# A graph attention layer: some of the gathered rows are loaded one by one from SP's queue

## The chip, the cores and the metric

The kernel runs on one core of a Trainium2 chip. A core has a matrix engine (PE, TensorE), a vector engine (DVE), a scalar engine (ACT), a general engine (POOL, GpSimd) and a sequencer for transfers (SP, SyncE). Each has its own queue of instructions, works it off in order, and waits on semaphores for the others. Transfers between the memory outside (DRAM) and the memory on the core (SBUF, 128 partitions) run on 16 DMA engines; SP, ACT and POOL start them. The metric is the device time of one execution in microseconds (us).

## The reference

One layer of graph attention over 12500 nodes and 412500 edges that are sorted by their target node. Cut to what matters:

```python
h = relu(layernorm(x)) @ W_node.T           # per node, 4 heads of 32
e = edge_attr @ W_edge.T                    # per edge
att = leaky_relu(sum([h[src], h[tgt], e] * a))
m = max(segment_max(att, tgt), 0)
ex = exp(att - m[tgt])
denom = segment_sum(ex, tgt) + (E - deg) * exp(-m)
out = x + segment_sum(ex / denom[tgt] * h[src], tgt)
```

The costly access is `h[src]`: for each of the 412500 edges a row of its source node, at an address that only the data tells.

## The kernel before

First a table is made in DRAM, one row per node: 144 floats (576 bytes) that hold h of the four heads, two columns of ones each, and the parts of the attention that belong to source and target. Then the edges are worked through in 58 batches. A batch has 8 chunks of 896 edges; a chunk has 7 tiles of 128 edges, so a full batch has 56 tiles (the last has 31; in all there are 3223).

Per batch, in the functions that follow:

- `index(b)` (L155) loads the batch's source and target indices, 128 partitions x 56 tiles each, from SP. It runs two batches ahead.
- `load(s)` (L404) starts from SP the edge features `eft` (L408), the target ids `mem` (L412, two loads), and eight small pieces of the table, `twb` (L418), whose addresses SP reads into registers first (`least_i`, L413).
- `gather(s)` (L431) lets POOL wait until `sums` is there (the copy to `gate`, L434) and then issues one indirect transfer per tile (L436): 128 rows of the table, one for each partition, at the 128 addresses in a column of `src`. The target is `hs`, a buffer that exists twice. `sums` belongs to the batch two before, whose `hs` buffer is used again.
- `begin(s)` (L445) multiplies `eft` and `mem` on PE into `z` (L454, L457) and makes the one-hot matrices `hot`. `eft` and `mem` have one buffer each, so the next `load` waits until these matmuls are done.
- `weigh(s)` (L478) takes the source part out of `hs` (L482, a transpose on DVE, which needs all rows of the batch) and computes the softmax weights with DVE and ACT. It reads `pen`, which `load_pen` (L440) loads from SP into a single buffer, after `weigh` of the batch before has read it.
- `scatter(s)` (L509) multiplies the rows by their weights (L520) and adds them up by target on PE (L527).
- `collect(s)` (L533) copies the sums out (L545), first of all the `sums` that POOL waits for (L537); `merge` joins two batches into `acc`.

The main loop (L688) gives the order by hand. In round b: the indices of batch b+2, `load` and `gather` of batch b+1, `weigh` of batch b, `load_pen` of batch b+1, `scatter` of batch b, `begin` of batch b+1, `collect` of batch b. `finish` adds x and stores an output part after some rounds. On SP's queue one round is therefore: two index loads, `eft`, two `mem`, the register load, eight `twb`, `pen`, and sometimes a store and a load of x.

A load that SP starts signals one of eight semaphores, which are taken in turn; the load that takes a semaphore again waits until the one eight before it has landed.

Of the kernel before, what the change touches and what calls it, by code (L numbers as in the profile page):

```python
# [12 lines left out]
I32 = mybir.dt.int32  # L13
AF = mybir.ActivationFunctionType
OP = mybir.AluOpType
AX = mybir.AxisListType
ENG = mybir.EngineType

P = 128
# [6 lines left out]
T = 7  # L26
CE = T * P
CT = 2 * T
NCH = -(-E // CE)
LAST = -(-(E - (NCH - 1) * CE) // P)  # L30
SB = 4
CB = 2 * SB
NBT = -(-NCH // CB)
# [8 lines left out]
NB = -(-N // P)  # L42
# [9 lines left out]
ROW = EROW + H  # L52
BUF = max(CE, MC * 2 * AW, CB * H * AW)
BANKS = 2
BIG = 2.0**100
EPS = 1e-5


def tiles_of(sc):

    return [T if c < NCH - 1 else LAST for c in (2 * sc, 2 * sc + 1) if c < NCH]
# [11 lines left out]
    return got  # L73


def groups_of(n):


    if n <= 4:
        return [(0, n, 0)]  # L80
    return [(0, 4, 0), (n - 4, 4, n - 4)]
# [3 lines left out]
def kernel(  # L85
    ctx: ExitStack,
    tc: tile.TileContext,
    x: bass.AP,
    src: bass.AP,
    dst: bass.AP,  # L90
    dstc: bass.AP,
    ef: bass.AP,
# [5 lines left out]
    nc = tc.nc  # L98
# [4 lines left out]
    table = dram.tile([NB * P, ROW], F32, name="table")  # L103
# [49 lines left out]
    indices = ctx.enter_context(tc.tile_pool(name="indices", bufs=3))  # L153

    def index(b):  # L155
        got = []
        for what, name in ((src, "src"), (dst, "dst")):
            t = indices.tile([P, SB * CT], I32, name=name)
            nc.sync.dma_start(t, what[:, b * SB * CT:(b + 1) * SB * CT])
            got.append(t)  # L160
        return got


    with (
# [13 lines left out]
        for g in range(NG):  # L178
            n = min(P, NC2 - g * P)
# [40 lines left out]
        def extent(g):  # L220
# [4 lines left out]
            pen = p2.tile([P, CE + 1], F32, name="pen", bufs=NG)  # L225
            nc.gpsimd.memset(pen, -BIG)
            yield
# [90 lines left out]
        early = []  # L318
        k = -4
        while k < 0 or line:  # L320
# [17 lines left out]
            if k == -2:  # L338
                early = [index(b) for b in range(2)]
# [2 lines left out]
            k += 1  # L342
        for _ in extents:
            pass
        pb = [pps.tile([P, NC2], F32, name=f"pb{k}", bufs=1) for k in range(2)]
        for k in range(2):
            for g in range(NG):
                n = min(P, NC2 - g * P)
# [35 lines left out]
        for a in range(4):  # L384
            r = slice(a * W, (a + 1) * W)
            nc.vector.tensor_scalar(nid[r, :], top[r, :].rearrange("p (b a) -> p b a", a=4)[:, :, a], rcol[r, :],
                                    None, op0=OP.add)
# [16 lines left out]
    def load(s):  # L404

        c0 = s.b * CB
        s.eft = work.tile([P, SB, CE], F32, name="eft")
        nc.sync.dma_start(s.eft, ef[s.b * SB:(s.b + 1) * SB, :, :].rearrange("j p e -> p j e"))  # L408
        s.mem = work.tile([P, 2, CE], F32, name="mem")
        for k in range(2):  # L410
            rows = dstc[c0 + 4 * k:c0 + 4 * k + 4, :]
            nc.sync.dma_start(s.mem[:, k, :].bitcast(I32), rows[:, None, :].to_broadcast([4, W, CE]))  # L412
        _, at = nc.values_load_multi_w_load_instructions(  # L413
            least_i[0:1, c0:c0 + CB], engines=[ENG.SP], min_val=0, max_val=NB * P - W,
            skip_runtime_bounds_check_because="a dst is at most N, and N + W at most NB * P")
        for i, v in enumerate(at):
            r = (i % 4) * W
            nc.sync.dma_start(twb[r:r + W, s.b % 2, i // 4, i * H:(i + 1) * H], table[ds(v, W), EROW:])  # L418
        s.hs = work.tile([P, SB * CT, ROW], F32, name="hs", bufs=2)
        s.tiles = []  # L420
        for t in range(T):
            for sc in range(s.b * SB, (s.b + 1) * SB):
                held = tiles_of(sc) + [0, 0]
                for c in range(2):
                    i = (sc - s.b * SB) * CT + c * T + t
                    if t < held[c]:
                        s.tiles.append(i)
                    else:
                        nc.vector.memset(s.hs[:, i, :], 0.0)

    def gather(s, sums=None):  # L431

        if sums is not None:
            nc.gpsimd.tensor_copy(gate, sums)  # L434
        for i in s.tiles:
            nc.gpsimd.indirect_dma_start(  # L436
                out=s.hs[:, i, :], out_offset=None, in_=table[:, :],
                in_offset=bass.IndirectOffsetOnAxis(ap=s.src[:, i:i + 1], axis=0))

    def load_pen(s):  # L440
        s.pen = work.tile([R, CE + 1], F32, name="pen")
        rows = pens[s.b * CB:(s.b + 1) * CB, :]
        nc.sync.dma_start(s.pen, rows[:, None, :].to_broadcast([CB, H, CE + 1]))
# [34 lines left out]
    def weigh(s):  # L478


        zst = work.tile([P, T, R], F32, name="zst")
        nc.vector.transpose(zst.rearrange("p t i -> p (t i)"),  # L482
                            s.hs[:, :, :EROW].rearrange("p (q t) (h k) -> p t q h k", t=T, h=H)[:, :, :, :, AW - 1])
        att = work.tile([P, BUF], F32, name="a")[:R, :CE]

        def grouped(what, g):
            return what.rearrange("r (t g i) -> r g t i", g=NQT, i=R)[:, g, :, :]

        for g in range(NQT):
            nc.vector.tensor_tensor(grouped(s.z, g), grouped(s.z, g), zst[g * R:(g + 1) * R, :, :], op=OP.add)  # L490
            nc.scalar.activation(grouped(att, g), grouped(s.z, g), AF.Identity, scale=0.2)  # L491
        nc.vector.tensor_tensor(s.z, s.z, att, op=OP.max)  # L492
        up = ps.tile([P, BANKS * 512], F32, name="up")[:R, :CE]
        nc.vector.tensor_tensor_scan(up, s.pen[:, :CE], s.z, 0.0, op0=OP.add, op1=OP.max)  # L494
        m = work.tile([P, BUF], F32, name="m")[:R, :CE]
        nc.vector.tensor_tensor_scan(m[:, ::-1], s.pen[:, CE:0:-1], up[:, ::-1], 0.0, op0=OP.add, op1=OP.max)  # L496
        nc.vector.tensor_tensor(att, s.z, m, op=OP.subtract)  # L497
        both = work.tile([P, 2, T, R], F32, name="both")
        for g in range(NQT):
            nc.scalar.activation(both[g * R:(g + 1) * R, 0, :, :], grouped(att, g), AF.Exp)  # L500
        for g in range(NQT):
            nc.vector.scalar_tensor_tensor(both[g * R:(g + 1) * R, 1, :, :], grouped(s.pen[:, 1:], g), -1.0 / BIG,  # L502
                                           grouped(m, g), op0=OP.mult, op1=OP.mult)
        s.ex, s.mx = exr
        for k, what in enumerate(exr):
            nc.vector.transpose(what.rearrange("p t r -> p (t r)"),
                                both[:, k, :, :].rearrange("p t r -> p (t r)"))
# [25 lines left out]
    def collect(s):  # L533

        n = s.chunks
        if s.b + 2 < NBT:
            nc.scalar.copy(sums, s.pa[:, CB // G - 1, 0:1])  # L537
        k = s.b % MB
        if k == 0:
            merged["r"] = work.tile([P, AW, MC + 1], F32, name="r")  # L540
        at = 1 + k * CB
        for g in range(min(n, G)):
            to = merged["r"][:, :, at + g:at + n:G]
            for h in range(H):
                nc.scalar.copy(to[h * W:(h + 1) * W, :, :],  # L545
                               s.pa[g * W:(g + 1) * W, :-(-(n - g) // G), h * AW:(h + 1) * AW]
                               .rearrange("p c d -> p d c"))
# [131 lines left out]
    def batch(b):  # L679
        if b not in batches:  # L680
            s = batches[b] = Batch()
            s.b = b
            s.chunks = min(CB, NCH - b * CB)
        return batches[b]

    stores = []
    with tc.manual_schedule():
        for b in range(-1, NBT):  # L688
            if b == -1:
                for k in range(2):  # L690
                    batch(k).src, batch(k).dst = early[k]
                load_pen(batch(0))
            elif b + 2 < NBT:
                batch(b + 2).src, batch(b + 2).dst = index(b + 2)
            if b + 1 < NBT:
                load(batch(b + 1))
                gather(batch(b + 1), sums if b >= 1 else None)
            if b >= 0:
                s = batch(b)
                weigh(s)  # L700
                if b + 1 < NBT:
                    load_pen(batch(b + 1))
                for store in stores:
                    store()
                stores.clear()
                scatter(s)
            if b + 1 < NBT:
                begin(batch(b + 1))
            if b >= 0:
                collect(batch(b))  # L710
                if (b + 1) % MB == 0 or b == NBT - 1:
                    g = b // MB
                    merge(g, min(MC, NCH - g * MC))
                del batches[b]
            if b == 3:
                count_windows()
            for b0, n, last in parts():
                if last == b:
                    stores.append(finish(work, ps, "up", em_ps, b0, n))
        for store in stores:  # L720
            store()
# [249 lines left out]
```

## Time and profile before

| | |
|---|---|
| time, median of 10 runs | 4199.71 us (4198.31 to 4200.48) |
| the profiled execution's own time | 4198.87 us |
| its span, first to last instruction | 4196.5 us |
| POOL busy | 3082.6 us (73%) |
| DVE busy | 1758.0 us (42%) |
| PE busy | 1110.6 us (26%), at a granted clock of 0.624 |
| ACT busy | 564.7 us (13%) |
| moved by DMA | 441.32 MB, mean 105 GB/s |
| by POOL's queue (gathers) | 237.83 MB, 21.6% of the 16 DMA engines' time |
| by SP's queue | 192.44 MB, 14.1% |

A row of the profile names the line, the engine, the operation and the tiles (written <- read), then count, busy time, mean duration and the idle time in front, with what ended it. Instructions with which SP starts a transfer are not counted as busy; they are shown in the time line and by line as SPq, their sequencer's queue, with the time that starting them took, not the transfer's. A wait names the instruction that ended it.

### The profile page before, as it was taken

Reading aid. Unit: us, or ns where it says so; the run is one execution under the profiler, and the core shown is the slowest. Engines: PE = TensorE matmul, PEld = TensorE weight load, DVE = VectorE, ACT = ScalarE, POOL = GpSimd, SP = SyncE. Lnnn points to the kernel's source line nnn. Section 1 sums busy time; section 2 is a strip of 40 time slices with the busy share of each in tenths; the row PEclk is TensorE's granted clock in tenths of the full one; section 3 lists DMA queues with packets and bytes.
Section 4 is the critical chain, followed back from the end, with each engine's and each line's share of the span. In section 5 each row is a group of like instructions: output and inputs, shape, how many; then the busy total and the mean of one; then the engine's idle time right before and its main releaser. Section 6 shows DMA issues by size and latency. Waiting matters only on the chain. (4 is left out here: it accounts for less than half of the span.)

```text
span 4196.5 us, 30865 instructions
## 1 busy us (share of the span) xinstructions
PE 1110.6 (26%) x8641; PEld 625.6 (15%) x8641; DVE 1758.0 (42%) x3450; ACT 564.7 (13%) x2149; POOL 3082.6 (73%) x3300
## 2 busy tenths in 40 slices
PE   6222222222222222222222223231222131313232
PEld 4011111111111111111111111111111111111111
DVE  7334453435343533343335333443343344433444
ACT  6011111111111111111111111111111111111111
POOL 2777777777777777777777777777777777777773
PEclk8566666566656565656566656565656565656566
DMA  5333433343433333434333334343333343433331
GB/s 165 110 114 89 130 98 113 93 118 89 118 93 114 98 114 93 118 88 118 93 114 98 114 93 118 89 118 94 113 98 114 93 118 89 118 93 114 98 115 40
DMA packets 243621, 441.32 MB, mean 105 GB/s; under 512 B 93914, under 2 KB 144086, under 8 KB 243446
## 3 DMA queue, kind: packets, MB, share of 16 engines
q0 software_dynamic: 103136, 237.83, 21.6%
q1 hardware_dynamic: 126486, 192.44, 14.1%
q10 hardware_dynamic: 13824, 9.02, 0.7%
q8 instruction: 72, 1.18, 0.1%
q14 instruction: 103, 0.84, 0.1%
HBM read 423.75 MB, written 15.29 MB: 105 GB/s over the span
## 5 line engine op out<-in xcount | busy, mean ns | idle before, releaser
L436 POOL DMA_INDIRECT hs<-table,src x3223 | 3049.0, 946 | 1056.3 <-issue 1052.0
L527 PE MATMUL pa<-hs,hot 128*32 128x140 f32 x6446 | 494.1, 341 | 2837.5 <-DVE hs L520 2808.4
L482 DVE STREAM_TRANSPOSE zst<-hs 128x224 f32<-128x224 f32 x58 | 33.6, 579 | 2003.4 <-DMA hs<-table,src 2003.4
L527 PEld LDWEIGHTS pa<-hs,hot 128*32 128x32 f32 x6446 | 408.7, 133 | 2946.6 <-DVE hs L520 2848.9
L520 DVE TENSOR_TENSOR hs<-hs,exr 128x924 f32<-128x924 f32 x461 | 478.0, 1108 | 50.7 <-ACT hs L514 50.7
L491 ACT ACTIVATE a<-z 32x224 f32<-32x224 f32 x232 | 80.3, 346 | 2364.5 <-DVE z L490 2364.5
L454 PE MATMUL z<-eft,wa 128*32 128x384 f32 (+1 forms) x928 | 361.9, 543 | 22.9 <-DMA twb<-table 22.9
L545 ACT COPY r<-pa 32x70 f32<-32x70 f32 x928 | 252.7, 272 | 27.8 <-PE pa L527 17.6
L457 PE MATMUL z<-mem,twb 128*32 128x512 f32 x464 | 186.3, 545 | 4.9 <-DVE key L465 4.9
L500 ACT ACTIVATE both<-a 32x224 f32<-32x224 f32 x232 | 89.9, 388 | 370.1 <-DVE a L497 365.9
L454 PEld LDWEIGHTS z<-eft,wa 128*32 128x32 f32 x928 | 97.7, 110 | 235.1 <-issue 228.8
L473 DVE TENSOR_TENSOR hot<-exr,key 128x448 f32<-128x448 f32 x231 | 128.0, 616 | 6.0
L490 DVE TENSOR_TENSOR z<-z,zst 32x224 f32<-32x224 f32 x232 | 89.8, 387 | 80.6 <-ACT a L491 75.2
L598 DVE TENSOR_TENSOR acc<-acc,a 128x70 f32 x461 | 107.4, 233 | 34.2 <-DVE acc L598 19.5
L494 DVE TENSOR_TENSOR_SCAN up<-pen,z 32x896 f32<-32x896 f32 x58 | 117.0, 2017 | 2.0
L496 DVE TENSOR_TENSOR_SCAN m<-pen,up 32x896 f32<-32x896 f32 x58 | 116.4, 2007 | 2.0
L502 DVE SCALAR_TENSOR_TENSOR both<-pen,m 32x224 f32<-32x224 f32 x232 | 88.1, 380 | 2.4
L537 ACT COPY sums<-pa 128x1 f32<-128x1 f32 x56 | 8.9, 159 | 580.9 <-PE pa L527 580.9
L663 PE MATMUL up<-a,ident 128*32 128x224 f32 (+2 forms) x480 | 44.9, 552 | 156.2 <-DVE a L656 156.2
L449 DVE TENSOR_SCALAR mem<-mem,nid 128x896 f32<-128x896 int32 x116 | 74.2, 680 | 21.3 <-issue 15.6
L492 DVE TENSOR_TENSOR z<-z,a 32x896 f32<-32x896 f32 x58 | 63.0, 1087 | 23.9 <-ACT a L491 23.9
L457 PEld LDWEIGHTS z<-mem,twb 128*32 128x32 f32 x464 | 51.4, 111 | 130.4 <-issue 110.0
(137 smaller groups left out, 860.7 us busy)
## 6 DMA issues: line engine op xcount, KB each, us to landing
eft<-in_ef SPq DMA_DIRECT2D x58, 1792.0 KB
mem<-in_dstc SPq DMA_DIRECT2D x116, 448.0 KB
hs<-table,src POOLq DMA_INDIRECT x3223
twb<-table SPq DMA_DIRECT2D x464, 0.5 KB
pen<-pens SPq DMA_DIRECT2D x58, 112.1 KB
table<-rows ACTq DMA_DIRECT2D x10, 648.0 KB
xg<-in_x SPq DMA_DIRECT2D x14, 448.0 KB
out<-xg SPq DMA_DIRECT2D x13, 448.0 KB
```

The costliest lines, as they stand in the source:

```text
L436: nc.gpsimd.indirect_dma_start(out=s.hs[:, i, :], out_offset=None, in_=table[:, :], in_offset=bass.IndirectOffsetOnAxis(ap=s.src[:, i:i + ...
L454: nc.tensor.matmul(s.z[:, part], wa3[:, j, :], s.eft[:, j, part], start=(j == 0), stop=False)
L457: nc.tensor.matmul(s.z[:, part], twb[:, s.b % 2, k, :], s.mem[:, k, part], start=False, stop=(k == 1))
L473: nc.vector.tensor_tensor(hot, rows_ps[:, None, :].to_broadcast([P, CT, W]), key[:, j * CT:(j + 1) * CT, None].to_broadcast([P, CT, W]), o ...
L490: nc.vector.tensor_tensor(grouped(s.z, g), grouped(s.z, g), zst[g * R:(g + 1) * R, :, :], op=OP.add)
L494: nc.vector.tensor_tensor_scan(up, s.pen[:, :CE], s.z, 0.0, op0=OP.add, op1=OP.max)
L496: nc.vector.tensor_tensor_scan(m[:, ::-1], s.pen[:, CE:0:-1], up[:, ::-1], 0.0, op0=OP.add, op1=OP.max)
L500: nc.scalar.activation(both[g * R:(g + 1) * R, 0, :, :], grouped(att, g), AF.Exp)
L520: nc.vector.tensor_tensor(rows, rows, s.ex[:, :n, q * H:(q + 1) * H, None].to_broadcast([P, n, H, HB]), op=OP.mult)
L527: nc.tensor.matmul(s.pa[g * W:(g + 1) * W, q // G, :], s.hot[j][:, c * T + i, :], s.hs[:, q * T + i, :EROW], start=(i == 0), stop=(i == n ...
L545: nc.scalar.copy(to[h * W:(h + 1) * W, :, :], s.pa[g * W:(g + 1) * W, :-(-(n - g) // G), h * AW:(h + 1) * AW] .rearrange("p c d -> p d c"))
L598: nc.vector.tensor_tensor(cols, cols, put[:, i0 + i, :, :], op=OP.add)
```

## The change

In three of four batches the last tile of the batch's list (in batch 0 too) is no longer gathered by POOL. SP loads its 128 rows one by one, each with a load of one partition of 576 bytes. 44 tiles, 5632 rows, are concerned. For them `index` also loads the tile's 128 source indices as a row into one partition (`row`, from the new input `srow`), and DVE multiplies them by 576 (`in_bytes`), so that they are byte addresses. SP reads 32 of them at a time into registers (`values_load_multi_w_load_instructions`) and then issues 32 loads.

The loads come from a generator, `singles`, and `load_singles(b, n)` issues the next n of them that belong to batches up to b. In round b there are up to 64 (two thirds of SR = 96) after `load` and `gather` of batch b+1; then what batch b still lacks, ahead of `weigh`; then 32 after `load_pen`. Before round 0, 96 are issued.

```diff
+SR = 96
+RL = 32
+def singled(b):
+    n = (b + 1) * SR // P - b * SR // P if b else 1
+    return tiles_in(b)[-n:] if n else []
...
+        rows = []
+        for i in singled(b):
+            c = b * SB * CT + i
+            t = indices.tile([1, P], I32, name="row")
+            nc.sync.dma_start(t, srow[c:c + 1, :])
+            rows.append((i, t))
+        got.append(rows)
         return got
+    def in_bytes(rows):
+        for _, t in rows:
+            nc.vector.tensor_scalar(t, t, float(ROW * 4), None, op0=OP.mult)
...
-        for i in s.tiles:
+        for i in tiles_in(s.b):
+            if i in singled(s.b):
+                continue
             nc.gpsimd.indirect_dma_start(
...
+    table_bytes = table.bitcast(U8).rearrange("n c -> (n c)")
+    def singles():
+        for b in range(NBT):
+            for i, t in batch(b).rows:
+                for p0 in range(0, P, RL):
+                    _, got = nc.values_load_multi_w_load_instructions(
+                        t[0:1, p0:p0 + RL], engines=[ENG.SP], min_val=0, max_val=(NB * P - 1) * ROW * 4,
+                        skip_runtime_bounds_check_because="a src is a node")
+                    for p, v in enumerate(got):
+                        nc.sync.dma_start(batch(b).hs[p0 + p:p0 + p + 1, i, :].bitcast(U8),
+                                          table_bytes[ds(v, ROW * 4)].rearrange("(o c) -> o c", o=1))
+                        yield
+    left = [(b, P * len(singled(b))) for b in range(NBT)]
+    def load_singles(b, n):
+        while n and left and left[0][0] <= b:
+            i, m = left.pop(0)
+            k = min(n, m)
+            for _ in range(k):
+                next(stream)
+            n -= k
+            if k < m:
+                left.insert(0, (i, m - k))
...
             if b + 1 < NBT:
                 load(batch(b + 1))
                 gather(batch(b + 1), sums if b >= 1 else None)
+                load_singles(b + 1, 2 * SR // 3 if b >= 0 else SR)
             if b >= 0:
                 s = batch(b)
+                load_singles(b, P)
                 weigh(s)
                 if b + 1 < NBT:
                     load_pen(batch(b + 1))
+                    load_singles(b + 1, SR // 3)
...
             if b >= 0:
+                if b + 2 < NBT:
+                    in_bytes(batch(b + 2).rows)
                 collect(batch(b))
```

The zeroing of tiles that the last batch doesn't fill is written differently but does the same.

More of the change, by code (lines that the diff above doesn't have):

```diff
@@ L54 @@
 BANKS = 2
+SR = 96
+RL = 32
+U8 = mybir.dt.uint8
 BIG = 2.0**100
@@ L73, in parts, with tiles_in @@
     return got
+def tiles_in(b):
+    got = []
+    for t in range(T):
+        for sc in range(b * SB, (b + 1) * SB):
+            for c, n in enumerate(tiles_of(sc)):
+                if t < n:
+                    got.append((sc - b * SB) * CT + c * T + t)
+    return got
+def singled(b):
+    n = (b + 1) * SR // P - b * SR // P if b else 1
+    return tiles_in(b)[-n:] if n else []
 def groups_of(n):
@@ L89 @@
     src: bass.AP,
+    srow: bass.AP,
     dst: bass.AP,
@@ L344 @@
             pass
+        for _, _, rows in early:
+            in_bytes(rows)
         pb = [pps.tile([P, NC2], F32, name=f"pb{k}", bufs=1) for k in range(2)]
@@ L419, in load @@
         s.hs = work.tile([P, SB * CT, ROW], F32, name="hs", bufs=2)
[L420 to L429, printed above, removed]
+        held = tiles_in(s.b)
+        for i in range(SB * CT):
+            if i not in held:
+                nc.vector.memset(s.hs[:, i, :], 0.0)
     def gather(s, sums=None):
@@ L686 @@
     stores = []
+    stream = singles()
     with tc.manual_schedule():
@@ L690 @@
                 for k in range(2):
-                    batch(k).src, batch(k).dst = early[k]
+                    batch(k).src, batch(k).dst, batch(k).rows = early[k]
                 load_pen(batch(0))
             elif b + 2 < NBT:
-                batch(b + 2).src, batch(b + 2).dst = index(b + 2)
+                batch(b + 2).src, batch(b + 2).dst, batch(b + 2).rows = index(b + 2)
             if b + 1 < NBT:
@@ L954 @@
         "src": np.ascontiguousarray(s.T),
+        "srow": s,
         "dst": np.ascontiguousarray(d.reshape(COLS, P).T),
```

## The prediction

> **What bounds the kernel now.** I read the page first, then the groups by line, then the time line of one batch (POOL, DVE, SP together), and last the waits of SP's queue. The page's chain of waits follows only the last 60 us, so it doesn't answer the question; the groups do.
>
> ```profile
> PE 1110.6 (26%) x8641; PEld 625.6 (15%) x8641; DVE 1758.0 (42%) x3450; ACT 564.7 (13%) x2149; POOL 3082.6 (73%) x3300
> L436 POOL DMA_INDIRECT hs<-table,src x3223 | 3049.0, 946 | 1056.3 <-issue 1052.0
> ```
>
> POOL issues 3223 gathers of 128 rows. Each takes 946 ns and is followed by some 302 ns in which POOL waits for nothing the profile shows: 1.248 us, and 3223 of them are 4022 of the 4196.5 us span. No other engine is over 42% busy. One batch looks like this (start, duration, engine and line):
>
> ```profile
> 2005.37 0.19 POOL L434 COPY gate<-sums 128x1 f32<-128x1 f32 x1
> 2007.09 0.58 DVE L482 STREAM_TRANSPOSE zst<-hs 128x224 f32<-128x224 f32 x1 [23.01 <-DMA hs<-table,src]
> 2018.77 0.77 SPq L443 DMA_DIRECT2D pen<-pens  x1
> 2031.09 0.16 ACT L537 COPY sums<-pa 128x1 f32<-128x1 f32 x1 [10.36 <-PE pa L527]
> 2036.60 0.38 SPq L408 DMA_DIRECT2D eft<-in_ef  x1
> 2042.12 14.56 SPq L418 DMA_DIRECT2D twb<-table  x8
> 2077.05 0.58 DVE L482 STREAM_TRANSPOSE zst<-hs 128x224 f32<-128x224 f32 x1 [43.70 <-DMA hs<-table,src]
> ```
>
> L482 opens `weigh` of a batch. From one to the next are 69.96 us, which are the 56 gathers. The gate's `sums` is ready at 2031.1, while POOL needs it only at about 2075: POOL has 44 us in hand before a late `weigh` holds it. SP looks idle, but its queue is in order and its waits say at which points:
>
> ```profile
> SPq L443 <- DVE exr L506: 1724.8, 56, 32.8
> SPq L408 <- PE z L454: 854.0, 55, 17.1
> SPq L418 <- DMA mem<-in_dstc: 686.8, 116, 7.6
> ```
>
> `pen` waits for `weigh` (11.7 us after its start, 2007.09 to 2018.77); `eft` waits until `begin`'s matmuls have read the old one (29.5 us after `weigh`'s start, 2007.09 to 2036.60); and the last two of eight `twb` loads wait for the `mem` transfers. From `eft`'s issue to the last `twb` are 20.1 us (2036.60 to 2042.12 + 14.56).
>
> **What it takes away.** 44 tiles (one each in three of four batches) leave POOL: 44 x 1.248 = 54.9 us, the most that can be gained.
>
> **What a row costs SP.** No row load of one partition is in the trace. Nearest is `twb`, also a small load at a register address:
>
> ```profile
> 2042.12 2.91 SPq L418 DMA_DIRECT2D twb<-table  x6
> 2050.59 6.09 SPq L418 DMA_DIRECT2D twb<-table  x2
> L418 SPq FUSED_REGOPS  x464: 46/46/56, 115.7 to 4085.1; - x155
> L418 SPq MOVE twb<-table x464: 29/29/43, 115.8 to 4085.2; - x155
> L418 SPq DMA_DIRECT2D twb<-table x464: 315/316/1034, 115.9 to 4090.5; - x155
> L413 SPq TENSOR_LOAD <-least_i x58: 810/1048/1075, 114.6 to 4073.2; - x58
> L593 DVEq TENSOR_LOAD <-q x58: 593/597/852, 287.6 to 4181.2; - x58
> L933 SPq TENSOR_LOAD <-total x1: 287/287/287, 469.0 to 469.0; - x1
> L933 DVEq TENSOR_LOAD <-total x1: 316/316/316, 4187.3 to 4187.3; - x1
> ```
>
> Six unhindered issues take 2.91 us, so one per (2.91 - 0.316) / 5 = 0.519 us: three instructions of 391 ns and three gaps of 43. The changed kernel has the byte address ready from DVE, so FUSED_REGOPS and its gap (89 ns) fall away: 0.43 us a row. Bounds: 0.316 (the DMA instruction alone, everything else overlapped) and 0.519 (nothing saved); a load with one descriptor could also be cheaper than any row here, which only the first rival takes up. Every 32 rows need a load of 32 registers. SP's line took 1.048 us for 8 and 0.287 for 1, so 109 ns a register and 3.66 for 32; DVE's 0.597 and 0.316 give 40 ns and 1.56. SP's own row is nearer, but its slope hangs on one sample, so I take 3.0, above the middle. A group of 32 rows, R, is then 32 x 0.43 + 3.0 = 16.8 us, with ends at 11.7 (0.316 and 1.56) and 20.3 (0.519 and 3.66).
>
> The eight semaphores that SP's loads take in turn let a row start only when the eighth before it has landed. The gather's landing in the chain is the nearest row:
>
> ```profile
> 4145.67 2.47 DMA hs<-table,src
> ```
>
> 2.47 / 8 = 0.31 us, under 0.43: it doesn't decide, until a landing takes 3.4 us.
>
> The Trainium skill, "Runtime: NRT & Kernel Launch", section "Instruction fetch mechanics", puts a register load at about 200 ns per register even in bulk. SP's row, 131 ns each for eight with everything in, is cheaper; by the page's figure a group would be 13.8 + 6.4 = 20.2 us (an estimate) and the sum below some 600 us more. "DMA: Bandwidth & Descriptors", section "Rules for kernel authors", advises to coalesce small transfers, since under 64 KB one pays mostly overhead: it speaks against this change, which cuts 73.7 KB gathers into 576-byte rows; the rows above agree in kind, since 128 rows are 4 x 16.8 = 67 us of SP where POOL spent 1.248 us; the sum already holds it.
>
> **Where the rows stand in SP's queue.** The built order shows: after `eft`, `mem`, `twb` come 64 rows; then what the batch about to be weighed still lacks; then `pen`, which waits for `weigh`; then 32 rows. Supply is 96 rows a batch, but a batch with a single tile needs 128, so the stream falls behind: counting it out, before `weigh` of batch b the rows of that batch that stand after `twb` are 0, 32, 64 and 96 for b mod 4 = 0, 1, 2, 3. They can't start before `twb` is out, 51 us into POOL's 70, so in the last two cases `weigh` starts late; a late `weigh` delays `pen`, then `begin`, then `eft`, and SP stands still meanwhile. POOL's 44 us cover a first such delay; after that SP and `weigh` form a loop of their own.
>
> **The loop over four batches**, from `weigh` of a batch with b mod 4 = 3 to the next such:
> - wait for `begin`: 29.5;
> - four times `eft` to last `twb`: 80.4. (In the first batch, where they are issued back to back, it is 112.77 to 134.16, so this is transfer time and stays.)
> - twelve groups of 32 rows: 12 x 16.8 = 201.6;
> - `pen` and the index loads between, three times 0.77 + 0.37 + 0.43 + 0.37 for the new index row, with gaps 2.4: 7.2;
> - `weigh` to `pen` where SP waits for it, once: 11.7;
> - two landings in front of a late `weigh`, 2.5 each: 5.0.
>
> Sum 335.4 us, against 4 x 69.96 = 279.8 before: 55.6 more. In the two other batches of the four `weigh` is far enough when SP reaches `pen`, so they add no wait. With smaller groups they do: SP then also waits for `begin` behind the batches with 32 and 64 late rows, and the path is 3 x 29.5 + 80.4 + 2.4 + 3 x 2.5 + 9R = 178.8 + 9R, which is the longer one below R = 15. POOL needs 221 x 1.248 = 276 and waits at its gate (L434); behind it stand all gathers of the batch after next, and `weigh` waits for those, but less long than for the rows.
>
> From batch 3 to 55 are 13 such periods: 723 us. The start: 96 rows before anything else and 32 more behind the next `twb` put the first `weigh` at 225 instead of 184.5, and the fourth, by the same steps, at 523 instead of 394: 128 more. The end, 55 to 57: one `twb` stretch with 64 + 32 + 32 rows, 120 us instead of 109: 11. The x loads and output stores of `finish` (0.40 and 0.41 us, 15 of each) lie in the same queue: 13. Sum 875 us; on the profiled 4198.87 that is 5074, and the median, 4199.71, stands as near. **Forecast: 5070 us.**
>
> **Costed at nothing.** The 44 multiplies on DVE are one-partition operations like its 0.19 us copies, 8 us in all, inside the 23 us in which DVE waits for `hs` before L482; if DVE were on the path they would cost that. The bytes are the same and the DMA engines are 35 to 37% busy. Nothing of PE or ACT changes.
>
> **Rivals.**
> - *SP keeps up, faster.* At R = 10.9 (0.25 us a row with 3.0) the loop is 178.8 + 98.1 = 277, as long as POOL's 276, and what the periods gain pays for the start; under R = 10 the full 54.9 us are gained: 4145. For it: one descriptor instead of 64. Against: `eft` with 512 pieces takes 0.38 us and `twb` with 32 takes 0.316, so the size hardly shows in the issue. 16%.
> - *SP-bound, but cheap.* At R = 11.7 the period is 284 (13 x 4.3 = 56 more), and start and end add some 50: 4305; at 13.3 it is 298.5 (243 more) and they add 75: 4515; and from 4250 with R a little under the lower end. For it: the gaps may overlap. 16%.
> - *Landing decides.* Rows land in 5 us because other transfers stand in the same rings (the stall in `twb` ends with `mem`'s landing, 14 us after `eft`'s issue): 5 / 8 = 0.63 a row, R = 23, 12 x 6.4 x 13 = 1000 more: about 6070. Against: `mem` has landed before the rows start. 5%.
> - *No change,* since SP just matches POOL or the rows aren't moved: the order has 5632 row loads and 44 fewer gathers, so only the first can be. 2%.
> - The forecast's mechanism with R from 13.3 to 20: 61%, 4515 to 5620 (R = 20: 12 x 3.2 x 13 = 500 above 5070, and the start).
>
> The range 4250 to 5620 leaves out the faster case, no change and most of the landing case. Faster by over 0.2% (8 us, about what ten runs can tell): 0.16; within: 0.02; slower: 0.82.
>
> **What would show it.** POOL's gathers stay at 946 ns but with idle time at L434's gate, released by `sums`; the wait of L482 names `hs` with the row loads as the last to land; SP's row loads at a pitch of 0.43 us and register loads of 3 us; distances of L482 uneven by fours, 335 us in sum. If L434 never waits, or row loads stand at 0.25 us, the forecast is wrong; if the pitch is right and the period isn't, the queue's order is misread.

## The result, and the profile after

The changed kernel takes 4500.54 us (median of 8 runs, 4496.9 to 4506.58), the kernel before 4199.57 us (28 runs in all). The ratio is 1.0718, with an interval of 1.0709 to 1.0727: 301 us slower, where 870 were forecast. The profiled execution has a span of 4506.8 us, 310 more than before, at a granted clock of 0.616 (0.624 before).

The page of the changed kernel, first the span and the busy times, then the groups that answer to those shown of before (line, engine, operation, tiles, count | busy us, mean ns | idle us in front and what ended it):

```profile
span 4506.8 us, 42844 instructions
PE 1112.5 (25%) x8641; PEld 628.5 (14%) x8641; DVE 1768.1 (39%) x3494; ACT 565.3 (13%) x2149; POOL 3050.4 (68%) x3256
L467 POOL DMA_INDIRECT hs<-table,src x3179 | 3016.9, 949 | 1057.9 <-issue 1031.2
L541 DVE STREAM_TRANSPOSE zst<-hs 128x224 f32<-128x224 f32 x58 | 33.4, 577 | 2304.0 <-DMA hs<-table 1263.2
L463 POOL COPY gate<-sums 128x1 f32<-128x1 f32 x56 | 10.9, 194 | 295.7 <-ACT sums L596 283.8
```

The two rows of before that answer to the last two:

```profile
L482 DVE STREAM_TRANSPOSE zst<-hs 128x224 f32<-128x224 f32 x58 | 33.6, 579 | 2003.4 <-DMA hs<-table,src 2003.4
L434 POOL COPY gate<-sums 128x1 f32<-128x1 f32 x56 | 11.1, 198 | 0.2
```

POOL issues 44 gathers fewer, at 949 ns instead of 946, and is busy for less of a longer span. Where the time went is in the last two rows. The transpose that opens `weigh` (L541, L482 before) is now released mostly by `hs<-table`, which without `src` behind it is a row load from SP. And POOL's gate, which before had 0.2 us of idle time in front of it, waits 283.8 us for `sums` (L463, L434 before). POOL is no longer what sets the pace.

The same in the time line of one period of four batches, `weigh`'s first instruction on DVE (start, duration):

```profile
2014.10 0.58 DVE L541 STREAM_TRANSPOSE zst<-hs 128x224 f32<-128x224 f32 x1
2103.39 0.58 DVE L541 STREAM_TRANSPOSE zst<-hs 128x224 f32<-128x224 f32 x1 [62.68 <-DMA hs<-table,src]
2181.88 0.58 DVE L541 STREAM_TRANSPOSE zst<-hs 128x224 f32<-128x224 f32 x1 [31.52 <-DMA hs<-table,src]
2272.97 0.58 DVE L541 STREAM_TRANSPOSE zst<-hs 128x224 f32<-128x224 f32 x1 [64.90 <-DMA hs<-table,src]
2313.23 0.58 DVE L541 STREAM_TRANSPOSE zst<-hs 128x224 f32<-128x224 f32 x1
```

The distances are 89.3, 78.5, 91.1 and 40.3 us, 299.1 in sum, where four batches took 279.8 before. The batches with late rows (rows that SP starts only behind the `twb` loads of the round in which their batch is weighed) wait for them; the one without (b mod 4 = 0) follows 40 us after the one before it, since its gathers are long done.

The names in the three brackets contradict this: they put the wait down to a gather (`hs<-table,src`), as the profile does for 21 of the 46 waits of L541. SP's row loads and POOL's gate in the same period show that these names mislead:

```profile
2068.19 0.19 POOL L463 COPY gate<-sums 128x1 f32<-128x1 f32 x1
2091.14 10.29 SPq L482 DMA_DIRECT2D hs<-table  x32
2136.99 0.20 POOL L463 COPY gate<-sums 128x1 f32<-128x1 f32 x1
2156.60 23.28 SPq L482 DMA_DIRECT2D hs<-table  x64
2206.11 0.18 POOL L463 COPY gate<-sums 128x1 f32<-128x1 f32 x1 [0.23 <-ACT sums L596]
2235.07 35.95 SPq L482 DMA_DIRECT2D hs<-table  x96
```

The gate stands behind the last gather of the batch that is weighed next. So the gathers of the three batches were out 35, 45 and 67 us before `weigh` started, and the last of the 32, 64 and 96 late rows 2 us before. In the whole run `weigh` starts 1.1 to 2.1 us after its last row load is out in all 44 batches that have one, and 27 us or more after its last gather.

SP's queue, by line (count, min/median/max ns, first and last start), and then in the round around 2014:

```profile
L478 SPq TENSOR_LOAD <-row x176: 1866/2124/2548, 134.8 to 4438.5; - x176
L482 SPq MOVE hs<-table x5632: 29/29/39, 136.8 to 4451.3; - x195
L482 SPq DMA_DIRECT2D hs<-table x5632: 224/228/321, 136.9 to 4451.4; - x195
L453 SPq DMA_DIRECT2D twb<-table x464: 315/316/1503, 116.7 to 4398.4; - x155
```

```profile
2003.43 0.39 SPq L443 DMA_DIRECT2D eft<-in_ef  x1
2006.44 1.20 SPq L447 DMA_DIRECT2D mem<-in_dstc  x2
2008.95 18.11 SPq L453 DMA_DIRECT2D twb<-table  x8
2029.14 23.36 SPq L482 DMA_DIRECT2D hs<-table  x64
2052.61 0.74 SPq L502 DMA_DIRECT2D pen<-pens  x1
2055.89 10.61 SPq L482 DMA_DIRECT2D hs<-table  x32
```

A row load costs SP 228 ns where a `twb` load costs 316. The 32 rows at the end take 10.61 us, so one per (10.61 - 0.228) / 31 = 0.335; the median distance over the whole run is 0.323. The stretch of 64 rows has one register load in its middle (2.12 us at the median). R, a group of 32 rows with its register load, is 12.8 us; the forecast had 16.8. From `eft` to the last `twb` are 23.6 us in this round, 21.4 in the mean (20.1 was taken).

SP's waits (where it waits <- what ends it: us in all, times, longest):

```profile
SPq L453 <- DMA mem<-in_dstc: 674.3, 115, 8.0
SPq L502 <- DVE exr L565: 418.5, 42, 14.3
SPq L443 <- PE z L513: 255.2, 40, 16.5
```

L443, `eft` waiting for `begin`, occurs 40 times over 55 batches, close to three times in four. That is the second path of the forecast, 3 x 29.5 + ... + 9R, and not the first, which waits there once in four.

The whole difference, from the starts of `weigh`: from batch 3 to batch 55 the mean period of four is 298.4 us (280.4 before), 13 x 18.0 = 234 more. Batch 3 starts at 470.0 (394.7 before), 75.3 more; 55 to 57 take 104.2 (109.0), 4.8 less; after the last start come 53.6 (48.2), 5.4 more. The sum is 310, as in the span.

### The profile page after: what moved, and what is told of

Its sections match the earlier page's. It is cut to its first block, busy times and chain, and to the rows that moved or that the text cites. A ratio compares the mean times of both kernels' runs of the same rounds, so it can differ in the third digit from the quotient of the medians.

```text
span 4506.8 us, 42844 instructions
## 1 busy us (share of the span) xinstructions
PE 1112.5 (25%) x8641; PEld 628.5 (14%) x8641; DVE 1768.1 (39%) x3494; ACT 565.3 (13%) x2149; POOL 3050.4 (68%) x3256
## 4 chain that ended last, share of the span: by engine, by line
POOL 26%; SPq 18%; issue 14%; DVE 13%; DMA 12%; PE 9%; ACT 4%; DVEq 0%; ACTq 0%; POOLq 0%
POOL hs L467 26%; SPq L482 14%; DMA mem<-in_dstc 10%; PE pa L586 5%; SPq L478 3%; DVE hs L579 3%; PE z L513 3%; DVE up L553 2%; DVE m L555 2%; DMA hs<-table,src 1%; PE z L516 1%; ACT both L559 1%; DVE z L549 1%; ACT a L550 1%; DMA hs<-table 1%
## 5 line engine op out<-in xcount | busy, mean ns | idle before, releaser
L467 POOL DMA_INDIRECT hs<-table,src x3179 | 3016.9, 949 | 1057.9 <-issue 1031.2
L541 DVE STREAM_TRANSPOSE zst<-hs 128x224 f32<-128x224 f32 x58 | 33.4, 577 | 2304.0 <-DMA hs<-table 1263.2
L463 POOL COPY gate<-sums 128x1 f32<-128x1 f32 x56 | 10.9, 194 | 295.7 <-ACT sums L596 283.8
```

What stands on the lines that cost most here:

```text
L467: nc.gpsimd.indirect_dma_start(out=s.hs[:, i, :], out_offset=None, in_=table[:, :], in_offset=bass.IndirectOffsetOnAxis(ap=s.src[:, i:i + ...
```

## The experiments

Three theories stood before the runs. Theory 1: it is the place of the late rows, behind the `twb` stretch and in front of `pen`, that makes SP and `weigh` a loop with waits in it. Theory 2: SP simply has too much to issue. Theory 3: the row loads disturb the other transfers. All ratios are against the kernel before, measured beside it on the same chip. All times are medians.

**All rows of a batch one batch ahead.** `e1_all_ahead` issues the same 5632 loads, but none of them late:

```diff
-                load_singles(b + 1, 2 * SR // 3 if b >= 0 else SR)
+                load_singles(b + 1, P)
...
-                    load_singles(b + 1, SR // 3)
```

> The same 5632 row loads, but all 128 rows of batch b+1 are issued in round b right after its twb loads, none after pen, so no row is still missing when its batch's weigh is due. Theory 1 (late rows: a row of the batch about to be weighed stands behind the 21 us from eft to the last twb, and the late weigh then holds eft): the loop is gone, POOL's 44 saved gathers show, 4145 us. Theory 2 (SP simply has too much to issue, in whatever order): 4500. Theory 3 (row loads disturb other transfers): 4500.

Measured: 4158.00 us, ratio 0.9900 (0.9883 to 0.9916). The same work of SP, and 42 us faster than before instead of 301 slower. The gate shows nothing any more:

```profile
L463 POOL COPY gate<-sums 128x1 f32<-128x1 f32 x56 | 11.0, 197 | 0.2
```

The period is 276.5 us, and POOL's 221 gathers at 1.248 are 275.8. Theory 2 falls for SR = 96. In the profiled execution, the slowest of the four, 21 us are missing to the full 54.9, and nearly all of them lie at the start: batch 3 begins `weigh` at 409, where four gathers fewer would put it near 390.

**One line moved.** `e5_late_first` issues the late rows ahead of `eft`, `mem` and `twb` instead of behind them. The quotas stay 64 rows behind `twb` and 32 behind `pen`; but the late rows no longer count against the 64, so they become 32 in each of three batches, where the changed kernel had 32, 64 and 96. Its expectation calls the numbers of rows unchanged; for the late ones that isn't so. The edit:

```diff
             if b + 1 < NBT:
+                if b >= 0:
+                    load_singles(b, P)
                 load(batch(b + 1))
...
-                load_singles(b, P)
                 weigh(s)
```

> As the changed kernel with one line moved: the rows that the batch about to be weighed still lacks are issued ahead of eft, mem and twb of the round instead of behind them; numbers of rows, and where the others stand, unchanged. If the place behind the twb stretch is the cause, these rows are out some 20 us before weigh is due and the loop is gone: 4147 by the same sum, or 4158 as the run with all rows ahead. If it is enough that SP has 96 rows a batch in this split, 4500.

Measured: 4161.44 us, ratio 0.9908 (0.9891 to 0.9924), period 275.7, nothing at the gate. The time line of SP, two stretches of it:

```profile
2012.88 10.22 SPq L482 DMA_DIRECT2D hs<-table  x32
...
2027.80 10.81 SPq L482 DMA_DIRECT2D hs<-table  x32
2038.71 0.41 SPq L443 DMA_DIRECT2D eft<-in_ef  x1
2039.23 1.21 SPq L447 DMA_DIRECT2D mem<-in_dstc  x2
2041.75 19.28 SPq L453 DMA_DIRECT2D twb<-table  x8
```

Late rows, in front of `eft`, fall into the time in which SP would wait for `begin` anyway. The `twb` stretch is as long as ever (21.0 us in the mean), but nobody's rows stand behind it. The move is worth 339 us, with the same 5632 loads. It changes the place and the number of the late rows together; `e4_mem_by_row`, below, leaves both as they were.

**The rows beside the work.** In `e2_beside` POOL gathers all tiles again, and SP still issues every row load, into a spare buffer that nobody reads:

```diff
-            if i in singled(s.b):
-                continue
...
-                        nc.sync.dma_start(batch(b).hs[p0 + p:p0 + p + 1, i, :].bitcast(U8),
+                        nc.sync.dma_start(spare[p0 + p:p0 + p + 1, :].bitcast(U8),
```

> POOL gathers all 3223 tiles again, and SP issues the same 5632 row loads at the same places of its queue into a spare buffer that nobody reads, so weigh never waits for a row. Theory 1: nothing waits for the rows, SP's own work fits beside the 70 us of POOL, 4200. Theory 2: SP's queue still delays eft, mem, twb and pen, 4500. Theory 3: the gathers or landings get longer, clearly over 4200, up to 4500.

Measured: 4199.72 us, ratio 1.000 (0.9991 to 1.001). 5632 more transfers, the 176 register loads and DVE's 44 multiplies change nothing as long as `weigh` doesn't wait for them. That rules theory 3 out (the gathers take 947 ns), and confirms the multiplies' price of nothing.

**A dearer row.** `e3_regops` gives back the address arithmetic that the change had put on DVE, so each row has one more instruction on SP:

```diff
-            nc.vector.tensor_scalar(t, t, float(ROW * 4), None, op0=OP.mult)
+            pass
...
-                        nc.sync.dma_start(batch(b).hs[p0 + p:p0 + p + 1, i, :].bitcast(U8),
-                                          table_bytes[ds(v, ROW * 4)].rearrange("(o c) -> o c", o=1))
+                        nc.sync.dma_start(batch(b).hs[p0 + p:p0 + p + 1, i, :], table[ds(v, 1), :])
```

> As the changed kernel, but the addresses are row numbers that SP multiplies itself (one more register operation for each row, 46 ns and a gap, about 0.08 us, so a group of 32 rows takes 15.4 instead of 12.8 us). Theory 1: the path 178.8 + 9R plus 5 grows by 9 x 2.6 = 23 us in each of 13 periods, with start and end some 350 more: 4850. Theory 2: 5632 x 0.08 = 460 more: 4960. Theory 3: unchanged, 4500.

Measured: 4928.28 us, ratio 1.1741 (1.1722 to 1.1761). This lies between the 4850 of theory 1 and the 4960 of theory 2, nearer to the latter, so the time alone doesn't tell them apart.

```profile
L481 SPq FUSED_REGOPS  x5632: 37/37/47, 137.6 to 4871.1; - x195
L481 SPq DMA_DIRECT2D hs<-table x5632: 224/225/286, 137.7 to 4871.2; - x195
SPq L442 <- PE z L511: 202.0, 13, 16.5
```

37 ns and its gap put the median distance from 0.323 to 0.408 us, and R from 12.8 to 15.5. The period goes to 326.9, 28.5 more, and the whole kernel is 428 us slower than the changed one. Nine groups of 2.7 would give 24.5. But above R = 15 the forecast's first path, with twelve groups, is the longer one: 335.4 - 201.6 + 12 x 15.5, and 5 for the longer `twb` stretch, is 325. This was worked out after the run; it puts both paths of the forecast within 2 us of a measured period. The last row agrees: `eft` (L442) waits for `begin` 13 times, once in four batches as on the first path, where the changed kernel waited 40 times.

**A shorter `twb` stretch.** SP's last two `twb` loads wait for `mem`. `e4_mem_by_row` loads `mem` as eight broadcasts of one row instead of two of four rows:

```diff
-            rows = dstc[c0 + 4 * k:c0 + 4 * k + 4, :]
-            nc.sync.dma_start(s.mem[:, k, :].bitcast(I32), rows[:, None, :].to_broadcast([4, W, CE]))
+            for j in range(4):
+                row = dstc[c0 + 4 * k + j:c0 + 4 * k + j + 1, :]
+                nc.sync.dma_start(s.mem[j * W:(j + 1) * W, k, :].bitcast(I32), row.to_broadcast([W, CE]))
```

> As the changed kernel, but mem is loaded by eight transfers of 32 partitions from one row each instead of two of 128 from four rows. If the two are slow because they run on few of the DMA engines, the stretch from eft to the last twb falls from 21 to about 14 us. Theory 1: 4 x 7 us less in each period, 270 us, which is under POOL's 276: POOL bounds again, 4150 to 4160. Theory 2: SP issues six more loads a batch, 4 x 6 x 0.4 = 10 us more a period, 4630, unless the stretch counts as SP's work. Theory 3: 4500.

Measured: 4177.20 us, ratio 0.9949 (0.9932 to 0.9965).

```profile
2026.45 0.38 SPq L443 DMA_DIRECT2D eft<-in_ef  x1
2029.46 5.66 SPq L448 DMA_DIRECT2D mem<-in_dstc  x8
2036.10 3.98 SPq L454 DMA_DIRECT2D twb<-table  x8
2042.11 18.11 SPq L483 DMA_DIRECT2D hs<-table  x48
```

The stretch is 14.0 us in the mean instead of 21.4. Four times 7.4 would put the loop at 269, below POOL's 276, and the measured period is 275.9: POOL sets the pace again, though the late rows stand where they stood. The 17 us over the expected 4160 lie at the start: batch 3 starts at 432.4, against 394.7 before. So the changed kernel's loop was longer than POOL's by 22 us in 298, and either of two things, the place of the rows or the stretch, decides whether the change gains or loses. `e7_before_mem` makes the same edit to the kernel before:

> The kernel before with mem loaded by eight transfers of one row each, and nothing else. The stretch from eft to the last twb falls from 21 to 14 us, but no row stands behind it and POOL sets the time: 4200. If the shorter mem transfers help by themselves, below 4190.

Measured: 4199.48 us, ratio 1.000 (0.999 to 1.0009), with the stretch at 14.0 us there too (21.6 without it). Where nothing waits behind it, the stretch is worth nothing.

**Fewer rows.** `e6_sr64` sets SR = 64, a tile in every other batch.

> SR = 64 in the changed kernel: a tile in every second batch (28 fewer gathers, 35 us to gain), rows in the same places, 42 after twb and 21 after pen. The steps of the loop with the prices measured now (R = 12.75, stretch 21.4) give at most 60 late rows in every second batch, a delay that POOL's 44 us cover, and SP idle enough to catch up: 18 us less than before, 4182. If any late row costs its time, 28 batches x 15 us over 4165: 4580.

Measured: 4188.00 us, ratio 0.9972 (0.9962 to 0.9981), the 4182 of theory 1 within 6 us.

**More rows.** With SR = 128 every batch has one tile (7424 rows). `e8_ahead_mem_128` has it with all rows ahead and `mem` by rows; `e16_ahead_mem_128` is the same kernel on another chip, beside `e14_ahead_128` (without the edit to `mem`), `e15_ahead_mem_96` (SR = 96) and `e13_before_look` (the kernel before). What was expected of e8, e13, e14, e15 and e16, in this order:

> SR = 128, a single tile in every batch (58 fewer gathers, 72 us to gain), all its rows issued right after twb of the round before, and mem loaded by eight transfers. SP needs 14 + 4 x 12.75 + 3 = 68 us a batch, POOL 55 x 1.25 = 69: both just fit, 4200 - 72 and about 15 lost at the start, 4140. If SP's waits for pen and begin come on top, it turns into the bound: 4200 to 4300.

> The kernel before, unchanged, for its profile in this call. 4200 if nothing disturbs; if it takes 5300 again, its profile shows where 19 us a batch go.

> As e9_ahead_128: 4500 if SP's own work (75.3 us a batch against POOL's 69) is a bound of its own; 4145 if only late rows cost time.

> As e10_ahead_mem_96: 4158 if what e1_all_ahead lacks to 4145 lies at the start; 4146 if it comes from the stretch in every batch.

> The same kernel as e8_ahead_mem_128, as a control for this call: 4145 again, if the kernel before takes 4200 here.

| kernel | us | ratio |
|---|---|---|
| e8, SR 128, ahead, `mem` by rows | 4145.21 | 0.9877 (0.9861 to 0.9894) |
| e16, the same | 4153.35 | 0.9885 (0.9869 to 0.9902) |
| e15, SR 96, ahead, `mem` by rows | 4159.98 | 0.9898 (0.9882 to 0.9915) |
| e14, SR 128, ahead | 4525.47 | 1.0770 (1.0752 to 1.0788) |
| e13, before | 4204.35 (one run; the median of seven others there is 4202.91) | |

e14 has no late row, and yet it is slower than the changed kernel. Its gate and SP's round say why:

```profile
L463 POOL COPY gate<-sums 128x1 f32<-128x1 f32 x56 | 10.3, 183 | 261.2 <-ACT sums L596 254.0 <-DMA hs<-table 5.4 <-DMA twb<-table 1.5
```

```profile
2001.51 0.39 SPq L443 DMA_DIRECT2D eft<-in_ef  x1
2002.00 1.25 SPq L447 DMA_DIRECT2D mem<-in_dstc  x2
2004.56 17.04 SPq L453 DMA_DIRECT2D twb<-table  x8
2023.69 48.85 SPq L482 DMA_DIRECT2D hs<-table  x128
2072.64 0.73 SPq L502 DMA_DIRECT2D pen<-pens  x1
2073.69 0.38 SPq L180 DMA_DIRECT2D src<-in_src  x1
...
2075.01 0.39 SPq L443 DMA_DIRECT2D eft<-in_ef  x1
```

```profile
SPq L453 <- DMA mem<-in_dstc: 598.6, 113, 6.7
SPq L453 <- DMA eft<-in_ef: 117.8, 58, 5.7
```

SP goes from one `eft` to the next in 73.5 us (75.1 in the mean), while POOL's 55 gathers are 68.6. In SP's list of waits `eft` never waits for `begin` and `pen` never for `weigh`. What SP mainly waits for, 12 us a batch, is that its own `mem` and `eft` land, that is, that their data has arrived. Theory 2 is true there: SP's own round, its issues and these landings, is a second bound, and it begins to decide between 96 and 128 rows a batch. With `mem` by rows the stretch is 6 us shorter, SP's round falls below POOL's (e16's gate has 0.3 us of idle time), and the same 7424 rows gain 50 to 54 us. That version is the best found; against e15 it gains another 7 us where 14 gathers fewer would be 17.

e15 adds the edit of `mem` to e1. Batch 3 starts at 395.6 instead of 409, and the period is 276.9 instead of 276.5; the time doesn't change (42.9 us gained against 41.8). So e1's late start isn't where all of its missing 13 us went. In e15's profile 16 us are missing to 54.9: 6 at the start, 4 in the periods and 6 behind the last `weigh` (54.7 us instead of 48.2). What causes them is open.

**Two chips on which every kernel was slower.** `e9_ahead_128` and `e11_ahead_128_again` are e14's kernel, `e10_ahead_mem_96` and `e12_ahead_mem_96_again` e15's. What was expected of e9, e10, e11 and e12, in this order:

> SR = 128 with all rows ahead and mem as in the kernel before. No row is late, but SP's own work of a batch, 21.4 for the stretch, 4 x 12.75 for the rows and 3 for pen and indices, is 75.3 us against POOL's 69: if SP's work alone can become the bound, 57 x 5.2 over 4200 = 4500, with the gate of POOL waiting. If only late rows cost time, 4145.

> SR = 96 with all rows ahead and mem by eight transfers: neither late rows nor SP's work bind, and the 128 rows ahead of round 0 stay. 55 us gained less the start: 4158 as without the shorter mem transfers. If the missing 13 us of that run came from SP's stretch in every batch and not from the start, 4146.

> The same kernel as e9_ahead_128, since there the kernel before took 5309 us instead of 4200, so that no number of that run can be set beside the others. As there: if SP's own work of 75.3 us a batch (21.4 + 4 x 12.75 + 3) can become the bound against POOL's 69, 4500; if only late rows cost time, 4145.

> The same kernel as e10_ahead_mem_96, for the same reason. If the 13 us that e1_all_ahead lacks to 4145 lie at the start, 4158; if they come from SP's stretch in every batch, 4146.

Measured: 7719.28, 6838.80, 7663.92 and 6792.83 us. On these two chips the unchanged kernel before itself took 5309.15 (beside e9 and e10) and 5296.59 us, so they are not compared with the rest. In e9 the 128 rows take more than twice what they take in e14:

```profile
2024.15 110.59 SPq L482 DMA_DIRECT2D hs<-table  x128
```

For 74 us of this round (2032 to 2106), instructions of SP took about 0.7 us each with gaps of about 0.7, while POOL's gathers kept their 947 ns. What slowed SP there is open, and so is what slowed the kernel before, of which no profile exists from those chips.

## Why the prediction was right and wrong

*What bounds the kernel now:* right. e2 and e7 change SP's work and the transfers and not the time; e1 and e5 take gathers away and the period falls to POOL's 276.

*Where the rows stand in SP's queue:* right. The four distances of `weigh` are uneven as the count of late rows (0, 32, 64, 96) said, the last late row is out 2 us before `weigh`, the gate waits for `sums`, and e1 and e5 show with the same loads in other places that the place makes the loss.

*What a row costs SP:* this is the step that failed. It took `twb`'s 316 ns and its 43-ns gaps for a row (0.43 us with the MOVE), and 3.0 us for 32 registers. Measured are 228 ns, 0.323 us from row to row at the median (0.335 in the round shown), and 2.12 us. R is 12.8 instead of 16.8, close to the lower end of 11.7. The argument that carried the choice, that the size of a load hardly shows in its issue, came from loads of 32 and more partitions and doesn't hold for a load of one. The price of the register load was too near to SP's 8-register row; 2.12 lies nearer to DVE's bound of 1.56.

*The loop over four batches:* the mechanism was right, and the mis-sized R also chose the wrong one of its two paths. The forecast's 335.4 stood on the first, with twelve groups; the second, 178.8 + 9R, which the text gives for R below 15, is the one that ran. With R = 12.8 it is 294.0, and 4 x 1.3 for the longer `twb` stretch makes 299.2; 298.4 was measured. Of the excess over before per period 18.0 us remained of 55.6, and that times 13 is 234 instead of 723: 489 of the 569 us by which the forecast missed. Most of the rest is the start, 75 instead of 128; the end is 1 instead of 11, and the 13 for the x loads and stores don't show.

*POOL in hand, multiplies at nothing, landing that doesn't decide:* right. In e4 the rows of one batch in four come out some 16 us after its last gather and the period is still POOL's; e2 has the multiplies and not the time; and SP's list of waits in the changed kernel names no landing in front of a row load.

*The rivals:* "SP-bound, but cheap" came true, with R between its two worked points, 11.7 and 13.3. It had 16%, the chance of a corner. Its reason, that the gaps may overlap, is the smaller part: of the 0.108 us by which a row was cheaper (0.323 instead of 0.431), 0.088 are the shorter instruction, which stood under the first rival (there with 64 descriptors for a `twb` load, where the text beside it has 32 pieces), and 0.020 the gaps. The faster rival's condition, R = 10.9 or less, did not occur; e4 came to POOL's pace by the other term, the stretch. That R decides between 4145 and 5070 was in the text; that a shape never seen in the trace makes R the least known number should have kept the chance of the lower part of 11.7 to 20.3 higher.

## What to carry to other kernels

Work moved to an idle queue that is worked off in order must be placed before it is priced: look for what stands in front of each item, which wait holds that, and whether the item's consumer releases that wait. Here one line moved turned 301 us of loss into 38 of gain. Where such a loop's period is close to the old bound, a few us per group are multiplied by groups and periods, so the price of a shape that the trace doesn't show is worth a bound from a smaller load, not from the nearest larger one. And a queue that has room for an average round has its own end: 96 rows a batch fitted into SP's round, 128 only after its wait for `mem` had been shortened.

## What the runs showed of the hardware

- A one-partition load of 576 bytes takes SP 228 ns to start, a load of 32 partitions 316 ns, and the next row starts 0.323 us after the one before with a MOVE between.
- A load of 32 registers takes 2.12 us, 66 ns a register; the 8-register load had 131. The Trainium skill, "Runtime: NRT & Kernel Launch", section "Instruction fetch mechanics", puts it at about 200 ns a register even in bulk; here, from a tile in SBUF, it is a third of that.
- Loading `mem` as eight one-row broadcasts instead of two of four rows took the stretch up to the last `twb` from 21.4 to 14.0 us, with the same bytes and six more instructions. The Trainium skill, "DMA: Bandwidth & Descriptors", section "Rules for kernel authors", says that a transfer whose outermost dimension is under 16 runs on only so many engines; the measurement agrees with it in kind, but no view here was used to count the engines.
- A wait behind which nobody stands costs nothing: the same 7 us a batch were worth 0 in the kernel before (e7) and 323 us in the changed one (e4).
- SP's instructions at some 0.7 us each on two chips, as told above: open.
